# The last image of a two-layer attention kernel: output by plain stores of sums formed on chip instead of accumulating DMAs, and a reordered preparation

## The chip, the cores and the metric

The kernel runs on one core of one Trainium2 chip. A core has a matrix engine (PE, TensorE), a vector engine (DVE, VectorE), an activation engine (ACT, ScalarE), a general engine (POOL, GpSimd), and a queue engine (SP, SyncE) that issues most of the DMAs. Each engine works through its own instructions in order and waits on semaphores for the others. SBUF is the memory on the chip, PSUM the eight banks into which PE writes, and HBM, where inputs and outputs lie, is reached by DMA only. The metric is the time of one execution on the device in microseconds (us); lower is better.

## The reference

x has the shape (8, 512, 64, 64): eight images of 512 channels and N = 4096 positions. Two layers follow one another.

Layer 0 is softmax attention. With f = Wf x and pooled g = maxpool(Wg x), v = maxpool(Wh x) (1024 pooled positions):

```
s = f^T g;  beta = softmax(s);  o = v beta^T;  x1 = gamma * (Wv o) + x
```

Layer 1 is linear attention on x1, with the feature map delu(u) = 10 relu(u) + exp(10 min(u, 0)):

```
Qf = delu(wq x1);  Kf = delu(wk x1);  V = wv x1
KV   = sum over positions of Kf V^T
norm = 1 / (Qf^T (sum over positions of Kf + 1e-10))
out  = x1 + gamma * (Qf^T KV) * norm
```

Everything is float32. KV and the sum of Kf run over a whole image, so the addend of layer 1 (called C below) can be formed only when x1 of the whole image is known.

## The kernel before

The positions of an image are cut into 8 chunks of 512 (CH), 64 chunks in all (TOTAL), numbered s. A tile of a chunk has 128 partitions (channels within a group) and 4 groups (KT) of 512 positions: 1 MB. The function `step(s)` writes out one step of a software pipeline by hand: each piece of work is registered with a time inside the step, `at(t, fn, ...)`, and at the end of the step all pieces are issued in order of those times. The times only set the order in which instructions stand in each engine's queue. The loop runs over s from -9 to 71, and three images overlap in it:

- *A work* for chunk s + 9: the projections f, g and h of layer 0.
- *B work* for chunk s: the softmax attention of layer 0 (`attend`), the projection that turns the chunk's tile of x (`x_b[s]`, pool `xb`, one buffer) into x1 in place (`project`), its store to `out` by SP (line 534), and the features q and k of layer 1 (`features`, `features_exp`, `features_sum`). The q features of two chunks (a pair) lie in one tile, `qq[pair]`, half of the partitions each.
- For layer 1, x1 and the k features are turned so that positions lie on the partitions, and `gather` (line 621) adds k^T x1 of the chunk to G, which grows over an image. For all chunks but the last, x1 is turned by DMA transposes (`split_x`, `turn_halves`, `join_x`); for chunk 63, by PE (`turn_x`, line 601) with ACT copying the four results out of PSUM (line 604).
- *C work* for the image before: `start_kb` forms the matrix kb of the sums of the k features; `turn_G` turns G on PE (line 663), copies it on ACT (665) and adds its two halves into gT on DVE (671); `make_KV` multiplies it with wv, which `load_wv1` loads (638), into pkv (685), and DVE makes kv of it (691, 692); `normalize` forms the divisors of a pair on PE (703), positions along the free axis and repeated on 64 partitions, inverts all 128 x 512 of them on DVE (707) and scales qq (708); `finish` multiplies kv and qq into pa (732), ACT copies pa into a tile y of two channel groups of two chunks (735), and POOL issues a DMA of 1 MB that adds y to `out` in HBM (738).

For images 0 to 6 the C work lies under the steps of the following image. For image 7 nothing follows: after step 63 come steps 64 to 71 with C work alone, all four pairs normalized in step 64 at the times

```
at(3.6 if here else 0.2, turn_k, s - 1)
gather(s - 1, at, 0.3, 0.4)
turn_G(b_c, at, 21.2 if here else 6.0)
make_KV(b_c, at, 36.9 if here else 8.2)
for i, t in enumerate((5.79, 5.8, 12.0, 12.1)):
    normalize(pair + i, at, t, t + 1.3)
```

and finished in the odd steps 65 to 71, with two y buffers of pool `yc` and two more (`y_late`) in the buffer that held the softmax weights E. At the end a flag is read that decides whether the whole is run again in a general form; it is not in this data.

Of the kernel before, what the change touches and what calls it, by code (L numbers as in the profile page):

```python
# [35 lines left out]
F32 = mybir.dt.float32  # L36
U16 = mybir.dt.uint16
AF = mybir.ActivationFunctionType
ALU = mybir.AluOpType
# [10 lines left out]
def tile_two_attention_blocks(  # L50
# [113 lines left out]
    def run(ctx, general):  # L164
# [13 lines left out]
        def bank(name):  # L178
            return psum.tile([P, CH], F32, tag="m", name=name)

        def scratch(name):
            return temp.tile([P, CH], F32, tag="t", name=name)
# [25 lines left out]
        fgs, fs, vps = {}, {}, {}  # L208

        th, hs, es, sums, totals, rtots, te, os_, to, ns = ({} for _ in range(10))  # L210
        kTs, xTs, pks, qq, halves, turned_halves = ({} for _ in range(6))


# [381 lines left out]
            u = turned_halves[s, k].rearrange("p (h t) c -> p h t c", h=2)  # L595
            nc.scalar.copy(v[:, k], u)  # L596

        def turn_x(s, t):
            px = bank(f"px_{s}_{t}")
            for k in range(KT):  # L600
                nc.tensor.transpose(px[:, bass.ts(k, P)], x_b[s][:, k, bass.ts(t, P)], ident)
            if t == 0:
                xTs[s] = turned.tile([P, NT, C], F32, tag="xT", name=f"xT_{s}")
            nc.scalar.copy(xTs[s][:, t, :], px)

        def turn_k(s):
            pt = bank(f"pkT_{s}").rearrange("p (t n) -> p t n", n=P)
# [5 lines left out]
        def gather(s, at, t, t_out):  # L613

            b, j = divmod(s, NCHUNK)
            G, m = st[b]["G"], {}

            def product():
                pg = m["pg"] = bank(f"pg_{s}")
                for t in range(NT):  # L620
                    nc.tensor.matmul(  # L621
                        pg[half(t % 2), :], kTs[s][:, t, :], xTs[s][:, t, :],
                        start=(t < 2), stop=(t >= NT - 2),
                    )

            def out():
                if j == 0:
                    nc.vector.tensor_copy(G, m["pg"])
                else:
                    nc.vector.tensor_tensor(G, G, m["pg"], ALU.add)  # L630

            at(t, product)
            at(t_out, out)


        def load_wv1(b):
            w = st[b]["w_v1"] = yc.tile([P, KT, C], F32, tag="y", name=f"w_v1_{b}")
            nc.sync.dma_start(out=w, in_=wv1r)

        def start_kb(b):  # L640
# [56 lines left out]
        def normalize(pair, at, t, t_out):  # L697

            m = {}

            def product():
                m["pd"] = bank(f"pd_{pair}")
                nc.tensor.matmul(m["pd"], kb, qq[pair], start=True, stop=True)

            def out():
                rn = scratch(f"rn_{pair}")
                nc.vector.reciprocal(rn, m["pd"])
                nc.vector.tensor_tensor(qq[pair], qq[pair], rn, ALU.mult)

            at(t, product)  # L710
            at(t_out, out)

        def finish(pair, ks, at, t):

            b, jp = divmod(pair, NCHUNK // 2)
            m = {}

            def product():
                kv = st[b]["kv"]
                if b == B - 1 and ks[0] > 0:  # L720

                    if "late" not in st:
                        st["late"] = work1.tile([P, 2, 2, 2, CH], F32, tag="E", name="y_late")
                    y = st["late"][:, pair % 2]
                else:
                    y = yc.tile([P, 2, 2, CH], F32, tag="y", name=f"y_{pair}_{ks[0]}")
                m["y"] = y
                for i, k in enumerate(ks):
                    for e in range(2):
                        pa = bank(f"pa_{pair}_{k}_{e}")  # L730
                        hf = half(1 - e)
                        nc.tensor.matmul(  # L732
                            pa, kv[hf, bass.ts(k, P)], qq[pair][hf, :], start=True, stop=True
                        )
                        nc.scalar.copy(y[:, i, e, :], pa)  # L735

            def out():
                nc.gpsimd.dma_start(  # L738
                    out=outr[b, :, ks[0] : ks[0] + 2, bass.ts(jp, 2 * CH)],
                    in_=m["y"].rearrange("p k e n -> p k (e n)"), accum_op=ALU.add,  # L740
                )

            at(t, product)
            at(t + 3.4, out)


        def step(s):
            here, after = 0 <= s < TOTAL, 0 <= s + 1 < TOTAL
            a = s + LEAD
            b, j = divmod(s, NCHUNK)  # L750
            b_c = b - 1
            c_here = 0 <= b_c < B
            pair = (b_c * NCHUNK + j) // 2
            work = []

            def at(t, fn, *args):
                work.append((t, len(work), fn, args))

            if here:
                at(0.5, load_b, s)  # L760
            if 0 <= a and a + 2 < LEAD:
                at(0.0, load_a, a + 2)
            if LEAD <= a + 1 < TOTAL:
                at(38.5, load_a, a + 1)
            if c_here and j == 0:
                at(0.6, load_wv1, b_c)

            if here:
                attend(s, at, {
                    1: (0.0, None), 2: (1.7, 3.5), 3: (3.9, None), 6: (14.4, 16.1), 5: (16.2, 20.5),  # L770
                    7: (17.9, 21.8), 4: (19.6, 22.5),
                })
                at(-0.6, sums_of_e, s, 3)
                at(0.3, sums_of_e, s, 4)
            if 0 <= s - 1 < TOTAL:
                at(-0.5, features_exp, s - 1)
                at(-0.4, features_sum, s - 1)
                if s < TOTAL:
                    at(-0.45, join_x, s - 1, 1)
                    at(1.8, join_x, s - 1, 2)  # L780
                    at(2.3, join_x, s - 1, 3)
                at(3.6 if here else 0.2, turn_k, s - 1)
                if here:
                    gather(s - 1, at, 12.6, 13.5)
                else:
                    gather(s - 1, at, 0.3, 0.4)
            if c_here and j == 0:
                at(0.2, start_kb, b_c)
                turn_G(b_c, at, 21.2 if here else 6.0)
                make_KV(b_c, at, 36.9 if here else 8.2)  # L790
            if c_here and here and j == 0:
                normalize(pair, at, 5.6, 13.2)
            if c_here and here and j % 2 == 1 and j < NCHUNK - 1:
                normalize(pair + 1, at, 3.5, 4.9)
            if c_here and not here and j == 0:
                for i, t in enumerate((5.79, 5.8, 12.0, 12.1)):
                    normalize(pair + i, at, t, t + 1.3)
            if c_here and j % 2 == 1:
                finish(pair, (0, 1), at, 9.2)
                finish(pair, (2, 3), at, 10.9)  # L800
            if 0 <= a < TOTAL:
                a_h(a, at, 19.7, 30.8, 37.8)
                a_fg(a, at, 21.3)
            if 0 <= a - 1 < TOTAL:
                at(18.5, bias_v, a - 1)
                at(36.8, a_turn, a - 1)
                if a % NCHUNK == 0:
                    at(39.0, sums_of_v, (a - 1) // NCHUNK)
            if after:
                n = s + 1  # L810
                at(5.7, weigh_two, n, 0)
                at(7.5, weigh_two, n, 2)
                for m, t in ((2, 9.3), (4, 10.6), (6, 11.8), (8, 13.1)):
                    at(t, sum_of_e, n, m)
                at(16.1, total, n)
                at(17.0, invert, n)
                if not general:
                    at(21.5, look, n)
                at(24.3, normalize_block, n, 0, 1)
                at(26.0, normalize_block, n, 0, 0)  # L820
                at(27.3, normalize_block, n, 1, 1)
                at(29.2, normalize_block, n, 1, 0)
                at(33.6, sums_of_e, n, 1)
                at(36.0, sums_of_e, n, 2)
            if here:
                project(s, at, 24.8, 36.0)
                at(37.0, features, s)
                if s < TOTAL - 1:
                    for k in range(KT):
                        at(32.9 + k, split_x, s, k)  # L830
                        at(33.0 + k, turn_halves, s, k)
                    at(37.3, join_x, s, 0)
                else:
                    for t in range(NT):
                        at(40.4 + t * 0.45, turn_x, s, t)

            for _, _, fn, args in sorted(work, key=lambda w: w[:2]):
                fn(*args)

        load_a(0)  # L840
        load_a(1)
        for s in range(-LEAD, TOTAL + NCHUNK):
            step(s)

    ENGINES = {
# [53 lines left out]
```

## Time and profile before

| what | value |
|---|---|
| median of 3 runs | 2845.95 us (2843.32 to 2849.13) |
| the profiled execution: its own time | 2846.64 us |
| its span in the trace | 2844.9 us |
| busy: PE, DVE, ACT, POOL | 2695.6, 2144.2, 1516.6, 709.6 us |
| last PE work of the features of chunk 63 (pk) | 2764.31 to 2768.01 us |
| kv of the last image ready | 2794.05 us |
| first and last of the eight last accumulating DMAs issued | 2797.95, 2824.54 us |
| plain store of xb, issue to landing | 5.0 us |
| accumulating DMA of y, issue to landing | 11.2 us (the last four of y_late: 17.7 us) |

All times inside the trace are from the start of the span. In a line of the timeline stand the start, the time from the first start to the last end, engine and line, operation, out<-in, and the count, then in brackets how long the engine was idle before it and what ended that. One float32 matmul stands as two instructions. In a row of a table of stretches stand the busy times of the engines, then the granted clock of PE (1.00 is full), the busy share of the 16 DMA engines and the GB/s moved. In the chain of waits, "issue" is time for which the profile shows no wait.

### The profile page before, as it was taken

To read this page: it belongs to the slowest core of one execution; us is meant where nothing else is said; L and a number is where in the kernel's file an instruction comes from. 1 tells how busy PE (TensorE), PEld (TensorE's weight loads), DVE (VectorE), ACT (ScalarE), POOL (GpSimd) and SP (SyncE) were. 2 spreads that over 40 slices of the span, in tenths; PEclk is the share of its full clock that TensorE was granted. 3 is DMA by queue.
4 is the path that set the end of the run, shared out by engine and by line. 5 is a ranking of instruction groups with operands and counts; after the bars stand their busy time and mean duration, and the time that the engine had idled before them with its cause. 6 is when DMAs were issued, how large, how long until landed. Compare 5 with 4: busy or idle time off the path is not lost.

```text
span 2844.9 us, 30593 instructions
## 1 busy us (share of the span) xinstructions
PE 2695.6 (95%) x10928; PEld 1810.9 (64%) x10928; DVE 2144.2 (75%) x2982; ACT 1516.6 (53%) x2629; POOL 709.6 (25%) x552
## 2 busy tenths in 40 slices
PE   8899999999999999999999999999999999989984
PEld 6566666666666666666766666666666666655551
DVE  4678778777787777877777877877878777787752
ACT  2255555556556556556556556456555556655542
POOL 4312222222321223222231222322222222211111
PEclk9999999999999999999999999999999999999996
DMA  4143244455454446454455454445544445544456
GB/s 155 36 119 91 88 119 133 97 140 148 115 137 119 108 129 163 98 139 120 118 133 148 106 131 131 120 120 148 118 120 135 118 118 148 133 101 110 112 138 119
DMA packets 394434, 346.96 MB, mean 122 GB/s; under 512 B 274592, under 2 KB 275104, under 8 KB 394272
## 3 DMA queue, kind: packets, MB, share of 16 engines
q1 hardware_dynamic: 371712, 275.82, 34.4%
q0 software_dynamic: 17408, 67.11, 12.7%
q10 hardware_dynamic: 5152, 1.97, 0.3%
q8 instruction: 89, 1.46, 0.2%
q14 instruction: 73, 0.60, 0.1%
HBM read 144.58 MB, written 134.22 MB: 98 GB/s over the span
## 4 chain that ended last, share of the span: by engine, by line
PE 71%; DVE 10%; ACT 8%; issue 4%; DMA 2%; POOL 2%; DVEq 0%; POOLq 0%; ACTq 0%
PE M L444 22%; PE N L507 11%; PE H L283 11%; PE fg L239 7%; PE pk L554 6%; PE s L354 5%; ACT n L517 3%; PE pa L732 3%; DVE r L394 3%; ACT E L358 3%; DMA u<-w 2%; PE tot L401 2%; PE pg L621 2%; DVE r L392 2%; ACT w L583 1%
## 5 line engine op out<-in xcount | busy, mean ns | idle before, releaser
L520 POOL TENSOR_TENSOR xb<-xb,n 128x512 f32<-128x512 f32 x192 | 244.5, 1274 | 596.4 <-ACT n L517 542.9
L444 PEld LDWEIGHTS M<-T,S 128*128 128x128 f32 x1536 | 287.3, 190 | 115.9 <-issue 30.7
L596 ACT COPY xT<-u 128x1024 uint16<-128x1024 uint16 x252 | 336.1, 1343 | 44.3 <-DMA u<-w 42.7
L444 PE MATMUL M<-T,S 128*128 128x256 f32 x1536 | 359.7, 384 | 0.0
L583 ACT COPY w<-xb 128x1024 uint16<-128x1024 uint16 x252 | 244.8, 1042 | 157.3 <-DVE xb L528 157.3
L517 ACT ACTIVATE n<-N,gb_v 128x256 f32<-128x256 f32 x384 | 161.5, 473 | 308.5 <-PE N L507 308.4
L420 DVE TENSOR_TENSOR E<-E,rtot 128x1024 f32<-128x1024 f32 x256 | 304.7, 1213 | 2.4 <-ACT tot L411 1.6
L358 ACT ACTIVATE E<-s 128x512 f32<-128x512 f32 x512 | 257.6, 626 | 42.6 <-PE s L354 42.1
L523 DVE TENSOR_TENSOR xb<-xb,N 128x512 f32<-128x512 f32 x256 | 175.1, 684 | 129.8 <-POOL xb L520 127.5
L507 PE MATMUL N<-to,w_v 128*128 128x256 f32 x1024 | 251.3, 389 | 15.0 <-ACT n L517 10.7
L392 DVE TENSOR_TENSOR r<-E 128x1024 f32<-128x1024 f32 x64 | 78.4, 1225 | 226.6 <-ACT E L358 226.6
L554 PE MATMUL pk<-xb,w_kqk 128*128 128x512 f32 x512 | 235.9, 604 | 10.5 <-DVE xb L528 10.5
L738 POOL DMA_DIRECT2D out_dram<-y x60 | 72.3, 1206 | 678.0 <-ACT y L735 675.8
L354 PE MATMUL s<-f,g 64*128 64x512 f32 x1024 | 239.7, 603 | 0.7 <-ACT kT L611 0.6
L406 DVE RECIPROCAL rtot<-tot 128x512 f32<-128x512 f32 x64 | 215.4, 3365 | 27.6 <-PE tot L401 27.6
L410 ACT ACTIVATE tot<-tot 128x512 f32<-128x512 f32 x64 | 37.2, 582 | 371.6 <-DVE rtot L406 364.5
L507 PEld LDWEIGHTS N<-to,w_v 128*128 128x128 f32 x1024 | 190.0, 191 | 66.5 <-ACT n L517 40.3
L444 PE MATMUL M<-E,vT 128*128 128x256 f32 x1024 | 231.6, 379 | 0.5 <-ACT vT L331 0.5
L272 POOL TENSOR_TENSOR tha<-xa 128x512 f32<-128x512 f32 x58 | 77.0, 1327 | 619.6 <-PE M L444 605.8
L444 PEld LDWEIGHTS M<-E,vT 128*128 128x128 f32 x1024 | 194.5, 190 | 54.0 <-issue 19.8
L507 PE MATMUL N<-o,w_v 128*128 128x256 f32 x768 | 195.1, 390 | 30.2 <-ACT n L517 27.3
L239 PE MATMUL fg<-xa,w_fg 128*128 128x512 f32 x464 | 210.6, 597 | 0.0
(129 smaller groups left out, 4647.0 us busy)
## 6 DMA issues: line engine op xcount, KB each, us to landing
xb<-in_x_dram SPq DMA_DIRECT2D x64, 1024.0 KB, 7.1
out_dram<-xb SPq DMA_DIRECT2D x64, 1024.0 KB, 5.0
out_dram<-y POOLq DMA_DIRECT2D x60, 1024.0 KB, 11.2
xa<-in_x_dram SPq DMA_DIRECT2D x58, 1024.0 KB, 6.6
w_v<-in_L_conv_wv_dram SPq DMA_DIRECT2D x8, 1024.0 KB, 9.1
x_early<-in_x_dram SPq DMA_DIRECT2D x6, 1024.0 KB, 5.4
out_dram<-y_late POOLq DMA_DIRECT2D x4, 1024.0 KB, 17.7
u<-w SPq DMA_TRANSPOSE x252, 3.3
```

Source lines behind the costliest of these rows:

```text
L239: nc.tensor.matmul(fg, w_fg[:, k, :], x_a[a][:, k, :], start=(k == 0), stop=(k == KT - 1))
L283: nc.tensor.matmul(m[i], w_h7[i][:, k, :], th[a][i][:, k, :], start=(k == 0), stop=(k == hk - 1))
L354: nc.tensor.matmul(sc[e], g[half(e), i, :], fs[s][half(e), :], start=True, stop=True)
L358: nc.scalar.activation(es[s][:, 2 * i + e, :], sc[e], AF.Exp)
L420: nc.vector.tensor_tensor(b, b, r, ALU.mult)
L444: nc.tensor.matmul(m[i], v7[i][:, k, :], te[s][i][:, k, :], start=(k == 0), stop=(k == hm - 1))
L507: nc.tensor.matmul(a[:, k, :], w_v7[i][:, bass.ts(k, P)], b, start=not more and k == 0, stop=True, skip_group_check=more or k > 0,)
L517: nc.scalar.activation(u[:, k, :], m[1][:, k, :], AF.Identity, bias=gb_v0[:, c : c + 1])
L520: nc.gpsimd.tensor_tensor(of_x(*ij), of_x(*ij), u, ALU.add)
L554: nc.tensor.matmul(pk, w_kqk[:, i, e * D : (e + 2) * D], x_b[s][:, i, :], start=(i == 0), stop=(i == KT - 1),)
L583: nc.scalar.copy(w, x_b[s][:, k, :].bitcast(U16).rearrange("p (n h) -> p h n", h=2))
L596: nc.scalar.copy(v[:, k], u)
```

## The change

The C work of image 7 (chunks 56 to 63) gets functions of its own.

- x1 of chunks 56 to 62 is loaded back from `out` into tiles that are free by then: 56 into the `xa` buffer, 57 and 58 into eight small tiles w and u, 59 and 60 into T1 to T4, 61 and 62 into E. The loads stand on SP from the end of step 62 to the end of step 63. x1 of chunk 63 is still in its `xb` tile.
- The addend pa is added to x1 on the chip: three channel groups on DVE straight from PSUM, the fourth by an ACT copy and an add on POOL. Then SP stores the chunk with plain DMAs. The eight accumulating DMAs of this image and the y tiles in E go.
- The divisors are formed with positions on the partitions: 16 small matmuls of 2 columns, two reciprocals of 128 x 16, then a broadcast copy on ACT and four transposes on PE per pair, and one multiplication on DVE.
- The copies of the turned x1 of chunk 63 come after exp and relu, two of four on DVE. gT stands on DVE behind the small reciprocals and before the scaling of qq.
- wv for image 7 is loaded in step 60, into the tile of an earlier image's vT.

```diff
-        def turn_x(s, t):
-            px = bank(f"px_{s}_{t}")
-            for k in range(KT):
-                nc.tensor.transpose(px[:, bass.ts(k, P)], x_b[s][:, k, bass.ts(t, P)], ident)
-            if t == 0:
-                xTs[s] = turned.tile([P, NT, C], F32, tag="xT", name=f"xT_{s}")
-            nc.scalar.copy(xTs[s][:, t, :], px)
+        def turn_x(s):
+            pxs[:] = [bank(f"px_{s}_{t}") for t in range(NT)]
+            for t in range(NT):
+                for k in range(KT):
+                    nc.tensor.transpose(pxs[t][:, bass.ts(k, P)], x_b[s][:, k, bass.ts(t, P)], ident)
+
+        def copy_x(s):
+            xTs[s] = turned.tile([P, NT, C], F32, tag="xT", name=f"xT_{s}")
+            for t in range(NT):
+                if t < NT // 2:
+                    nc.vector.tensor_copy(xTs[s][:, t, :], pxs[t])
+                else:
+                    nc.scalar.copy(xTs[s][:, t, :], pxs[t])
...
+        def place(s, *tiles):
+
+            b, j = divmod(s, NCHUNK)
+            x_last[s] = []
+            for t in tiles:
+                k, n = len(x_last[s]), t.shape[1]
+                nc.sync.dma_start(out=t, in_=outr[b, :, k : k + n, bass.ts(j, CH)])
+                stored.setdefault(s, []).append((t, k, n))
+                x_last[s] += [t[:, i, :] for i in range(n)]
...
+        def divisors(pair):
+
+            if "d" not in late:
+                late["d"] = bank("d").rearrange("p (i t e) -> p i t e", t=NT, e=2)[:, 0 : NCHUNK // 2]
+            for t in range(NT):
+                nc.tensor.matmul(
+                    late["d"][:, pair % (NCHUNK // 2), t, :], qq[pair][:, bass.ts(t, P)],
+                    kb[:, 0:P:D], start=True, stop=True,
+                )
+
+        def invert_divisors(n):
+            if n == 0:
+                late["rd"] = small.tile([P, NCHUNK // 2, NT, 2], F32, tag="rd", name="rd")
+            i = slice(2 * n, 2 * n + 2)
+            nc.vector.reciprocal(late["rd"][:, i], late["d"][:, i])
+
+        def spread(pair):
+
+            u = scratch(f"u_{pair}")
+            r = late["rd"][:, pair % (NCHUNK // 2)].rearrange("p t e -> p (t e)")
+            nc.scalar.copy(
+                u.rearrange("p (i d) -> p i d", d=D), r.unsqueeze(2).to_broadcast([P, 2 * NT, D])
+            )
+            sp = late[pair] = bank(f"sp_{pair}")
+            for t in range(NT):
+                nc.tensor.transpose(sp[:, bass.ts(t, P)], u[:, bass.ts(t, P)], ident)
+
+        def scale(pair):
+            nc.vector.tensor_tensor(qq[pair], qq[pair], late[pair], ALU.mult)
+
+        def finish_last(pair, k):
+            b, jp = divmod(pair, NCHUNK // 2)
+            for e in range(2):
+                pa = bank(f"pa_{pair}_{k}_{e}")
+                hf = half(1 - e)
+                nc.tensor.matmul(
+                    pa, st[b]["kv"][hf, bass.ts(k, P)], qq[pair][hf, :], start=True, stop=True
+                )
+                x = x_last[2 * pair + e][k]
+                if k < KT - 1:
+                    nc.vector.tensor_tensor(x, x, pa, ALU.add)
+                else:
+                    y = scratch(f"y_{pair}_{e}")
+                    nc.scalar.copy(y, pa)
+                    nc.gpsimd.tensor_tensor(x, x, y, ALU.add)
+
+        def store_last(s):
+            b, j = divmod(s, NCHUNK)
+            for t, k, n in stored[s]:
+                nc.sync.dma_start(out=outr[b, :, k : k + n, bass.ts(j, CH)], in_=t)
...
+            first = TOTAL - NCHUNK
+            if s == TOTAL - 4:
+                at(30.0, load_wv1, B - 1)
+            if s == TOTAL - 2:
+                at(37.3, place_first, first)
+            if s == TOTAL - 1:
+                at(0.7, place_small, first + 1, "w")
+                at(5.0, place_small, first + 2, "u")
+                at(22.0, place_half, first + 3, "T2", "T3")
+                at(22.1, place_two, first + 5)
+                at(36.9, place_half, first + 4, "T1", "T4")
+            if s == TOTAL:
+                pairs = [first // 2 + i for i in range(NCHUNK // 2)]
+                x_last[s - 1] = [x_b[s - 1][:, k, :] for k in range(KT)]
+                stored[s - 1] = [(x_b[s - 1], 0, KT)]
+                at(-0.45, copy_x, s - 1)
+                at(0.1, turn_k, s - 1)
+                at(0.2, start_kb, B - 1)
+                gather(s - 1, at, 0.25, 0.35)
+                at(0.4, divisors, pairs[0])
+                at(0.5, divisors, pairs[1])
+                turn_G(B - 1, at, 0.6)
+                at(0.7, invert_divisors, 0)
+                at(0.8, divisors, pairs[2])
+                at(0.9, divisors, pairs[3])
+                at(1.1, invert_divisors, 1)
+                at(1.2, spread, pairs[0])
+                at(2.2, scale, pairs[0])
+                make_KV(B - 1, at, 3.0)
+                at(3.1, spread, pairs[1])
+                at(3.2, scale, pairs[1])
+                for i in range(2, 4):
+                    at(6.6, spread, pairs[i])
+                for i, p in enumerate(pairs):
+                    for k in range(KT):
+                        at(7.0 + 4 * i + k, finish_last, p, k)
+                    if i < 2:
+                        at(7.1 + 4 * i, scale, pairs[i + 2])
+                    at(10.5 + 4 * i, store_last, 2 * p)
+                    at(10.6 + 4 * i, store_last, 2 * p + 1)
...
-        for s in range(-LEAD, TOTAL + NCHUNK):
+        for s in range(-LEAD, TOTAL + 1):
```

`turn_G` registers its DVE part (gT) 1.5 after the time given to it, so at 2.1, and `make_KV` its DVE part (kv) 3.5 after, so at 6.5. The small functions that call `place` (`place_first`, `place_small`, `place_half`, `place_two`) only choose the tiles named above.

More of the change, by code (lines that the diff above doesn't have):

```diff
@@ L210, in run @@
         th, hs, es, sums, totals, rtots, te, os_, to, ns = ({} for _ in range(10))
+        pxs, x_last, stored, late = [], {}, {}, {}
         kTs, xTs, pks, qq, halves, turned_halves = ({} for _ in range(6))
@@ L636, in load_wv1 @@
         def load_wv1(b):
-            w = st[b]["w_v1"] = yc.tile([P, KT, C], F32, tag="y", name=f"w_v1_{b}")
+            if b < B - 1:
+                w = yc.tile([P, KT, C], F32, tag="y", name=f"w_v1_{b}")
+            else:
+                w = image.tile([P, KT, C], F32, tag="vT", name=f"w_v1_{b}")
+            st[b]["w_v1"] = w
             nc.sync.dma_start(out=w, in_=wv1r)
@@ L719, in product @@
                 kv = st[b]["kv"]
[L720 to L727, printed above, removed]
+                y = m["y"] = yc.tile([P, 2, 2, CH], F32, tag="y", name=f"y_{pair}_{ks[0]}")
                 for i, k in enumerate(ks):
@@ L744, in finish, with place_first @@
             at(t + 3.4, out)
+        def place(s, *tiles):
[6 more added lines that the diff above has]
+                x_last[s] += [t[:, i, :] for i in range(n)]
+        def place_first(s):
+            place(s, xa.tile([P, KT, CH], F32, tag="xa", name=f"x1_{s}"))
@@ new lines, in place_small, with place_half, place_two @@
+        def place_small(s, tag):
+            place(s, *(
+                work1.tile([P, 1, CH], F32, tag=f"{tag}{k}", name=f"x1_{s}_{k}") for k in range(KT)
+            ))
+        def place_half(s, *tags):
+            place(s, *(work1.tile([P, 2, CH], F32, tag=t, name=f"x1_{s}_{t}") for t in tags))
+        def place_two(s):
+            e = work1.tile([P, MT, CH], F32, tag="E", name=f"x1_{s}")
+            place(s, e[:, 0:KT, :])
+            place(s + 1, e[:, KT:MT, :])
+        def divisors(pair):
[6 more added lines that the diff above has]
+                )
@@ new lines, in scale @@
+        def scale(pair):
[11 more added lines that the diff above has]
+                    nc.vector.tensor_tensor(x, x, pa, ALU.add)
+                else:
+                    y = scratch(f"y_{pair}_{e}")
+                    nc.scalar.copy(y, pa)
+                    nc.gpsimd.tensor_tensor(x, x, y, ALU.add)
@@ L764, in step @@
                 at(38.5, load_a, a + 1)
-            if c_here and j == 0:
+            if c_here and here and j == 0:
                 at(0.6, load_wv1, b_c)
@@ L781, in step @@
                     at(2.3, join_x, s - 1, 3)
-                at(3.6 if here else 0.2, turn_k, s - 1)
+                if here:
+                    at(3.6, turn_k, s - 1)
                 if here:
                     gather(s - 1, at, 12.6, 13.5)
-                else:
-                    gather(s - 1, at, 0.3, 0.4)
-            if c_here and j == 0:
+            if c_here and here and j == 0:
                 at(0.2, start_kb, b_c)
-                turn_G(b_c, at, 21.2 if here else 6.0)
-                make_KV(b_c, at, 36.9 if here else 8.2)
+                turn_G(b_c, at, 21.2)
+                make_KV(b_c, at, 36.9)
             if c_here and here and j == 0:
@@ L794, in step @@
                 normalize(pair + 1, at, 3.5, 4.9)
[L795 to L798, printed above, removed]
+            if c_here and here and j % 2 == 1:
                 finish(pair, (0, 1), at, 9.2)
@@ L833, in step @@
                 else:
-                    for t in range(NT):
-                        at(40.4 + t * 0.45, turn_x, s, t)
+                    at(40.4, turn_x, s)
+            first = TOTAL - NCHUNK
[38 more added lines that the diff above has]
+                    at(10.6 + 4 * i, store_last, 2 * p + 1)
             for _, _, fn, args in sorted(work, key=lambda w: w[:2]):
```

## The prediction

> **What bounds the kernel now.** I read the page first (PE busy 95% of the span), then the chain of waits. Over the span the chain is 71% PE; after the last main step it is something else:
>
> ```profile
> 2761.88 1.27 POOL xb L520
> 2763.14 34.78 issue
> 2797.93 0.02 POOLq L738
> 2797.95 1.20 POOL out_dram L738
> ...
> 2824.52 1.23 POOLq L858
> ```
>
> Columns: start, length, what. From 2763 on the chain does not follow PE's stream: it is a 35 us preparation, then POOL's eight accumulating stores. The change touches this stretch and a few DMAs before it, so the prediction is made for 2763 to 2844.9. What the engines do in it, in order of time:
>
> ```profile
> 2773.73 3.63 PE L621 MATMUL pg<-xT,kT 128*64 128x512 f32 x8 [0.46 <-ACT kT L611]
> 2778.45 3.36 DVE L707 RECIPROCAL rn<-pd 128x512 f32<-128x512 f32 x1 [0.36 <-PE pd L703]
> 2782.45 3.35 DVE L707 RECIPROCAL rn<-pd 128x512 f32<-128x512 f32 x1
> 2786.45 0.75 DVE L671 TENSOR_TENSOR gT<-g 128x256 f32<-128x256 f32 x2
> 2787.30 5.44 PE L685 MATMUL pkv<-w_v,gT 128*128 128x512 f32 x8 [7.59 <-issue]
> 2792.78 0.75 DVE L691 SCALAR_TENSOR_TENSOR kv<-b_v,ksum,pkv 128x512 f32<-128x512 f32 x1 [5.58 <-PE pkv L685]
> 2822.19 2.05 ACT L735 COPY y_late<-pa 128x512 f32<-128x512 f32 x4 [3.69 <-DMA out_dram<-y_late]
> ```
>
> G^T (L671) was ready to be formed at 2780.34, when ACT's copy of it ended, but stands on DVE behind two reciprocals of 3.36 us. PE is idle 7.6 us meanwhile. kv is ready at 2794.05. The last line shows ACT waiting for a y buffer that an accumulating DMA still reads: from 2797.95 the DMA sets the pace. Stretches of the same trace:
>
> ```profile
> core 0: us, PE busy (x) PEld busy (x) DVE busy (x) ACT busy (x) POOL busy (x), PEclk, DMA share, GB/s
> 2766.00:2767.50 1.50, 1.50 (x5) 0.65 (x4) 0.00 (x0) 0.00 (x0) 0.00 (x0) 1.00 1.03 362
> 2770.40:2773.80 3.40, 0.70 (x6) 0.49 (x8) 1.85 (x9) 2.35 (x5) 0.00 (x0) 1.00 0.45 167
> 2773.80:2777.20 3.40, 3.40 (x8) 0.67 (x8) 0.03 (x1) 0.00 (x0) 0.00 (x0) 0.50 0.00 0
> 2784.00:2787.50 3.50, 0.20 (x1) 0.23 (x2) 3.17 (x4) 0.00 (x0) 0.00 (x0) 0.51 0.00 0
> 2787.50:2790.90 3.40, 3.40 (x5) 1.33 (x6) 0.00 (x0) 0.00 (x0) 0.00 (x0) 0.50 0.00 0
> 2800.00:2841.00 41.00, 12.09 (x40) 5.34 (x36) 2.00 (x2) 11.80 (x24) 8.35 (x7) 0.64 1.04 205
> ```
>
> The engines of the DMA are full (share 1.04) at 205 GB/s while they accumulate; with the plain store of xb alone (2766.0 to 2767.5) they are as full at 362 GB/s. The 8.39 MB of accumulation take 41.7 us of DMA records (2799.72 to 2841.45, 5.2 us per MB), and from the last byte to the end of the span it is 3.4 us. The two half-clock rows show why pg and pkv are slow: pg is 8 in 1.94 us one step earlier, and pkv is 3.6 us on average for the seven images before.
>
> **What the Trainium skill says.** "DMA: Bandwidth & Descriptors", SWDGE vs HWDGE vs iDMA: accumulating is possible only in a DMA issued from GpSimd, a plain store may go from SP; "Issuing engines are not separate DMA queues": all share 16 engines. The trace agrees (the accumulation is on q0, everything of SP on q1), so what the change gains is the rate, not a second path. "TensorE: Matmul & The Clock Gate", Part 1: after an idle window of about 3.4 us the clock is halved, after a busy one it is full, and the windows run free. The trace agrees: 0.70 us busy in 3.4 was followed by clock 0.50. "SBUF — State Buffer", Who interferes with whom: a VectorE instruction with one SBUF input does not contend with GpSimd. The new adds read x1 from SBUF and pa from PSUM; the trace has no such pair side by side long enough to tell.
>
> **The change, part by part** (times on the clock of the trace before; pk of chunk 63 ends at 2768.0 in both).
>
> 1. Exp and relu go before the copies of x^T, and two of four copies go to DVE. Exp and relu take 1.30 us (2770.46 to 2771.76) and now end at 2769.35. DVE copies from 2768.54: 2 x 0.69 (the G copy, L628), overlapped by 0.05, so 2769.85. kk 0.69: 2770.55, before 2772.48. ACT's other two copies (2 x 0.51) end at 2770.4, under kk.
> 2. k^T 0.63 on PE, 0.4 on ACT, then pg. PE's gap is now about 2 us with 0.6 of work in it, before 4 with as little; I take the full clock: 1.94 us, end 2773.7 (half: 3.63). G added at 2774.5, before 2778.1.
> 3. Divisors of pairs 0 and 1 stand before G^T on PE: 8 matmuls of two passes each. No row has them; a transpose pass with a weight load is 0.12 us (16 in 1.91), a weight load of pd alone 0.19. 16 x 0.12 to 0.19 = 1.9 to 3.0, I take 2.4: 2776.1. pGT 0.6, ACT 0.6: 2777.35.
> 4. Before gT, DVE now has the second small reciprocal, which waits for pairs 2 and 3 on PE behind pGT: 2.4 more, 2779.1. A reciprocal of 16 elements a row is 16/512 of 3.36 plus the 0.15 of the smallest DVE rows: 0.25. gT 0.75: 2780.2, before 2787.2. So the wait on 6.7 us of reciprocals becomes one of about 2 us on small matmuls.
> 5. pkv: PE has been busy, so full clock, 3.6: 2783.9. Scaling of pair 1 stands before kv on DVE and waits for its transposes behind pkv: 0.6 + 0.7. kv 1.27: **2786.5, before 2794.05, 7.5 us earlier**. All 13.4 us of L707 go. The broadcast copies on ACT (0.5 to 1.3 each) lie under the divisors and pkv; the first would be seen only above 1.7.
> 6. Finish: 24 adds and 2 scalings on DVE at 0.65 (L523: two in 1.33), 17.2 us, ready at 2804.3; k=3 goes by ACT (0.51) and POOL (L520, 1.27), 10.2 us for eight, beside DVE. PE: 32 of 0.45. Chunk 56 needs six DVE operations and pa number 7: 2786.5 + 3.2 + 0.6 + 1.3 = 2791.6.
> 7. Stores: first data 0.9 after issue (xb: 2764.68 to 2765.59), 2792.6. 1.05 MB at 362 GB/s is 2.9; store and load together took 7.0 for two, 3.5. I take 3.1: 8 x 3.1 = 24.8, 2817.4. Chunks of pair p are ready every 4.6 us and drain in 6.2, so the DMA does not starve. With the 3.4 us of ending: **2820.8**.
> 8. Moved DMAs. x1 of chunk 56 now stands on SP before the load of xb 63: at most 3.8 us of delay (one load's records, 2742.91 to 2746.7). xb 63 then lands near 2750.5; POOL first needs it at 2757.06: hidden, 6.5 us to spare. The loads of 57 to 62 share the DMA with the two accumulations issued at 2746.8 and 2749.1: 7 loads, xb in and out at 3.1, and 12.1 of accumulation, from 2742.5: done by 2783, before 2787. Loads that wait for T2, T3 hold up on SP only other loads and the store of xb 63, which nobody reads until pair 3. w_v of the last image goes behind xb of step 60, 30 us before the next transposes: nothing, as it was hidden in the tail too (landed 2773, used 2787).
>
> Sum: kv 7.5; first data 7.1 earlier (2799.7 to 2792.6); drain 41.7 to 24.8, 16.9; together 24.0 off the span of 2844.9. The profiled run took 2846.64; the median is 2845.95, so I take the difference from the median: 2821.9.
>
> **Rivals.**
> *A, DMA drain with early kv* (above): 2822, own range 2816 to 2827 (2.8 to 3.5 us per MB). For it: full DMA in both kinds of row.
> *B, half clock in the preparation*: windows run free, so pg (+1.7) and pkv (+1.8 to 3.6) may be slow again, and the divisors may cost 0.19 a pass (+1.2): kv 2791 to 2793, time 2826 to 2828. Against: PE's gaps are shorter than in the row at 0.70.
> *C, x1 loads collide in step 63*: if xb 63 comes over 6.5 us late or the transposes of chunk 62 slow down, the step stretches by the rest; at half the DMA rate 3 to 6 us: 2825 to 2828. Against: SP's ring was empty from 2746.7 to 2765.6.
> *D, slower: stores serialized on SP.* If each waited for the one before to land: 5.0 per 1 MB store, by estimate 2.7 per quarter (2.0 of fixed time, 5.0 less 3.0, plus a quarter of 2.9) and 3.5 per half: 5 + 8 x 2.7 + 4 x 3.5 + 15 = 56 us from 2791.7, then the ending: about 2850 on the span, 2851. It decides against the change from 6.1 us per MB (2844.9 - 3.4 - 2792.6 = 48.9 for 8 MB). Against: in the built order a store waits for the eighth DMA before it, not the last.
> *E, no difference*: the gain would have to be spent elsewhere; nothing in the trace offers 24 us.
>
> **Chances.** A 0.74, B 0.12, C 0.09, D 0.03, E 0.02. Faster 0.95, same 0.02, slower 0.03; 0.2% (5.7 us, the spread of the three runs) is about what can be told. The range 2814 to 2829 takes in A with 2.7 us per MB and an earlier kv below, B and C above.
>
> **What will show it.** Right: gT right after the small reciprocals near 2780; L707 gone from the tail; kv near 2786.5; SP stores back to back with DMA share 1 at 330 to 370 GB/s; last byte about 3 us before the end. Wrong: PE clock 0.5 over pg or pkv; holes between the stores; DVE adds waiting for x1; step 63's first xb add after 2758.

## The result and the profile after

| | before | after |
|---|---|---|
| median of 4 runs, us | 2847.52 (2843.32 to 2849.13) | 2825.07 (2822.93 to 2826.77) |
| the profiled execution: its own time, us | 2846.64 | 2822.93 |
| its span, us | 2844.9 | 2821.1 |

The ratio is 0.9923 (95% interval 0.9906 to 0.994): 22 us faster. On the spans it is 23.8 us, against the 24.0 that were forecast. A second set of five runs of the changed kernel gave a median of 2822.18 beside a before of 2847.78, ratio 0.9914 (0.99 to 0.9927).

Until the last main step is over nothing has moved: pk of chunk 63 ends at 2768.83, before at 2768.01. In the kernels below that moment lies between 2765 and 2771, without order, so stretches of the tail are given **from the end of pk** ("pk +") wherever two kernels are compared.

The timeline of PE after the change, from the turned x1 of chunk 63 on (start, time from first start to last end, engine and line, operation, out<-in, count, in brackets the idle time before and what ended it):

```profile
2769.76 0.82 PE L603 MATMUL px<-ident,xb 128*128 128x128 f32 x6
2771.41 0.63 PE L616 MATMUL pkT<-ident,kk 128*128 128x128 f32 x4 [0.84 <-DVE kp L657]
2772.50 1.94 PE L628 MATMUL pg<-xT,kT 128*64 128x512 f32 x8 [0.46 <-ACT kT L618]
2774.37 1.95 PE L782 MATMUL d<-kb,qq 128*128 128x2 f32 x16
2776.18 0.64 PE L674 MATMUL pGT<-ident,G 128*128 128x128 f32 x4
2776.67 2.25 PE L782 MATMUL d<-kb,qq 128*128 128x2 f32 x16
2778.78 1.09 PE L802 MATMUL sp<-ident,u 128*128 128x128 f32 x4
2779.92 6.18 PE L696 MATMUL pkv<-w_v,gT 128*128 128x512 f32 x8
```

PE has no hole of over 0.9 us left up to pkv, pg is at its full-clock 1.94 us, and the reciprocals of 3.36 us are gone from before gT. But pkv, which starts 8.2 us earlier, takes 6.18 us, longer than the 5.44 of before. The table of stretches (busy time of PE, PEld, DVE, ACT, POOL, then PE's granted clock, DMA share, GB/s) says why:

```profile
2770.40:2773.80 3.40, 2.10 (x12) 0.90 (x12) 2.04 (x10) 1.89 (x4) 0.00 (x0) 1.00 1.05 392
2774.50:2778.00 3.50, 3.50 (x32) 3.41 (x32) 0.94 (x2) 1.15 (x3) 0.00 (x0) 1.00 1.01 391
2778.20:2785.00 6.80, 6.75 (x14) 3.46 (x14) 1.55 (x4) 1.40 (x3) 0.00 (x0) 0.50 0.01 5
2795.23:2818.77 23.54, 8.57 (x37) 4.98 (x33) 10.13 (x17) 3.42 (x6) 7.78 (x7) 0.79 0.98 361
```

PE's records fill 3.50 of 3.50 us in the second row, all of them divisors and pG^T, and yet PE's granted clock is at half in the third. That is looked into below. The last row is the whole drain: the DMA engines are full at 361 GB/s, where the accumulation was full at 205. The DMA table for 2785 to 2822, in 40 slices (tenths of busy share, then GB/s):

```profile
DMA  0000000000099999999999999999999999930000
GB/s 0 0 0 0 0 18 0 0 0 0 0 359 383 381 383 383 388 376 381 379 363 376 374 350 390 350 388 372 374 379 387 370 383 394 363 148 11 0 0 0
```

There is no hole between the first byte and the last: the eight chunks' stores run back to back. Chunk 56 is issued by SP at 2794.31 and its data starts at 2795.23; the last byte lands at 2818.77, 2.3 us before the end. The chain of waits no longer helps here. For this kernel it goes back only over the last adds and has 0.0% of the span:

```profile
2804.68 0.69 DVE xb L817
2805.37 0.34 POOLq L976
2805.71 0.69 POOL xb L821
```

It starts from POOL's last work (the add for chunk 63) and doesn't see that 12 us of plain stores are still under way. The end of this kernel is read from the DMA table.

From pk +, in us, all kernels of this document, each from one profiled execution ("end" is the start of the last instruction of the trace, 0.05 us before the span ends):

| kernel | pkv takes | kv ready | data of the drain: first, last | drain takes | end |
|---|---|---|---|---|---|
| before | 5.44 | 26.03 | 31.70, 73.43 | 41.73 | 76.79 |
| after | 6.18 | 19.61 | 26.40, 49.94 | 23.54 | 52.25 |
| after, again | 5.60 | 19.59 | 26.38, 49.95 | 23.57 | 52.25 |
| e1_prep_only | 5.01 | 19.57 | 24.98, 66.46 | 41.48 | 69.68 |
| e2_stores_only | 5.28 | 25.59 | 32.60, 58.53 | 25.93 | 61.06 |
| e3_gt_first | 3.63 | 21.35 | 27.18, 68.99 | 41.80 | 72.33 |
| e4_half_stored | 5.72 | 19.59 | 24.28, 39.30 | 15.03 | 46.87 |
| e5a_late_divisors | 4.78 | 15.87 | 25.42, 48.77 | 23.35 | 51.05 |
| e5b_filled | 3.60 | 14.88 | 24.43, 47.76 | 23.33 | 49.96 |
| e6_first_in_pieces | 5.63 | 19.59 | 22.43, 46.75 | 24.31 | 48.96 |
| e7_all | 3.60 | 14.88 | 17.73, 44.69 | 26.95 | 46.79 |
| e8_steady | 3.60 | 14.88 | 17.91, 45.17 | 27.27 | 47.77 |

The 24.5 us between the first two rows' ends are 5.3 of an earlier first byte, 18.2 of a shorter drain and 1.0 of a shorter ending.

### The profile page after: what moved, and what is told of

It is laid out like the page before. It is cut to its first block, busy times and chain, and to the rows that moved or that the text cites. A ratio compares the mean times of both kernels' runs of the same rounds, so it can differ in the third digit from the quotient of the medians.

```text
span 2821.1 us, 30743 instructions
## 1 busy us (share of the span) xinstructions
PE 2695.8 (96%) x10968; PEld 1817.2 (64%) x10968; DVE 2148.3 (76%) x3006; ACT 1506.6 (53%) x2607; POOL 709.9 (25%) x552
```

## The experiments

Theory A is the forecast's: the drain sets the end, its length is set by the kind of DMA, and the preparation only sets when it begins. The rival, P, looks for the larger part of the gain in the preparation. The first two runs do one half of the change each.

**The preparation alone.** From the changed kernel: no loads of x1, and the accumulating DMAs as before.

```diff
-                        at(7.0 + 4 * i + k, finish_last, p, k)
...
-                    at(10.5 + 4 * i, store_last, 2 * p)
-                    at(10.6 + 4 * i, store_last, 2 * p + 1)
+                    finish(p, (0, 1), at, 7.0 + 4 * i)
+                    finish(p, (2, 3), at, 8.0 + 4 * i)
```

> The changed preparation (copies after exp and relu, divisors with positions on partitions, G^T ahead of the scaling), but the eight accumulating DMAs of the kernel before. Theory A (the DMA drain sets the end, the preparation only says when it starts): kv about 5.6 us earlier than before, as in the changed kernel; the first y tile 3.9 us later; then 41.7 us of accumulation and 3.4 us of ending as before: span 2839 to 2840, 5 to 6 us below the 2844.9 of before, ratio about 0.998. Rival P (the preparation, with the 13.4 us of reciprocals taken off VectorE, is what gained): span 2821 to 2828.

Median 2840.86, ratio 0.9972 (0.9965 to 0.9979), 7.1 us, a little more than the 5 to 6 expected. kv comes 6.5 us earlier, the first data 6.7, and the end 7.1. The accumulation takes 41.48 us, as before (41.73), though it starts 6.7 us earlier.

**The stores alone.** The changed kernel with the old preparation: copies of the turned x1 on ACT before exp and relu, 128 x 512 divisors and reciprocals.

```diff
+                normalize(pairs[0], at, 5.79, 7.09)
+                normalize(pairs[1], at, 5.8, 7.1)
+                turn_G(B - 1, at, 6.0)
+                make_KV(B - 1, at, 8.2)
+                normalize(pairs[2], at, 12.0, 15.9)
+                normalize(pairs[3], at, 12.1, 19.9)
```

> x1 loaded back, adds on chip and plain stores as in the changed kernel, but the preparation of the kernel before (reciprocals of 128 x 512; those of pairs 2 and 3 stand on VectorE after the adds of pairs 0 and 1, so that the first stores don't wait for them). Theory A: kv at 2794 to 2795; first store data near 2800; VectorE has 8.1 us of reciprocal and scaling between the adds, so pairs 1 and 2 come every 8 us where the drain takes 6: last data near 2827, span 2829 to 2831, 14 to 16 us below before. Rival P: span not more than 7 us below before (2838 or more).

Median 2831.55, ratio 0.9943 (0.9927 to 0.996), 16.4 us by the medians and 15.7 in the tail. So the two halves give 7.1 and 15.7, together 22.8 of the 24.5: the stores carry two thirds of it, and A holds. The 1.7 left over lies in the drain: it takes 25.93 us here and 23.54 in the changed kernel, 2.4 more, of which the times of the first bytes take some 0.5 back. DVE in this run, from its timeline:

```profile
2797.59 3.68 DVE L814 TENSOR_TENSOR x<-x,pa 128x512 f32<-128x512 f32 x6 [1.50 <-PE pa L809]
2801.19 3.35 DVE L715 RECIPROCAL rn<-pd 128x512 f32<-128x512 f32 x1
...
2808.17 0.68 DVE L814 TENSOR_TENSOR x_T<-x_T,pa 128x512 f32<-128x512 f32 x1
2808.77 3.35 DVE L715 RECIPROCAL rn<-pd 128x512 f32<-128x512 f32 x1
```

The two reciprocals of pairs 2 and 3 stand between the adds, so sums come late and the DMA runs short:

```profile
2803.10:2829.00 25.90, 12.66 (x37) 6.38 (x36) 16.85 (x22) 3.47 (x6) 7.96 (x7) 0.76 0.89 327
```

A share of 0.89 at 327 GB/s over the drain, where the changed kernel has 0.98 at 361. With the accumulation the same kind of reciprocals cost the drain next to nothing: 41.73 us with them (before) and 41.48 without (e1_prep_only).

What "the stores" stands for is more than one thing. The accumulating DMAs add to HBM, are issued by POOL and move their 8.39 MB in 2176 packets; the plain ones are issued by SP and have 4352. No run changes one of these alone (a plain store issued by POOL, for one), so it is shown that the kind of DMA sets the rate, and not which of its traits does.

**One number.** How much of the preparation's 7.1 us was only the order of the work? The kernel before, with G^T ahead of the reciprocals:

```diff
-                turn_G(b_c, at, 21.2 if here else 6.0)
+                turn_G(b_c, at, 21.2 if here else 5.5)
```

> The kernel before with one number changed: turn_G of the last image at 5.5 instead of 6.0, so that the transposes of G stand before the divisors on TensorE and G^T before the reciprocals on VectorE. Theory A: G^T at about 2780; pkv then runs under the two reciprocals, which end near 2788; kv near 2789.4, 4.7 us earlier; the accumulations start that much earlier: span 2840, ratio about 0.998. A rival (the reciprocals of pairs 0 and 1 must come before the first pa anyway, so the order does not matter): kv and span as before within 1 us.

Median 2843.51, ratio 0.9985 (0.9976 to 0.9993): 4.5 us. Its timeline (PE and DVE):

```profile
2781.87 1.88 PE L703 MATMUL pd<-qq,kb 128*128 128x512 f32 x4
2782.69 0.76 DVE L671 TENSOR_TENSOR gT<-g 128x256 f32<-128x256 f32 x2 [1.37 <-ACT g L665]
2783.37 3.35 DVE L707 RECIPROCAL rn<-pd 128x512 f32<-128x512 f32 x1
2783.59 3.63 PE L685 MATMUL pkv<-w_v,gT 128*128 128x512 f32 x8
2791.35 0.74 DVE L691 SCALAR_TENSOR_TENSOR kv<-b_v,ksum,pkv 128x512 f32<-128x512 f32 x1
```

The reciprocals now run beside pkv instead of ahead of it. And pkv takes 3.63 us, the full clock: ahead of it stand the old divisors with 512 columns, not the new ones with two. What the full clock saves is lost again at L691, which waits on DVE for the second reciprocal until pk +20.1, 4.1 us after the last matmul of pkv.

**The half clock.** Is it the two-column matmuls? Two runs on the changed kernel. The first thins them out ahead of pkv (pair 1's go beside pG^T, those of pairs 2 and 3 behind pkv):

```diff
-                at(0.5, divisors, pairs[1])
+                at(0.65, divisors, pairs[1])
...
-                at(0.8, divisors, pairs[2])
-                at(0.9, divisors, pairs[3])
-                at(1.1, invert_divisors, 1)
+                at(3.15, divisors, pairs[2])
+                at(7.05, divisors, pairs[3])
+                at(7.06, invert_divisors, 1)
```

with the scalings of pairs 1 to 3 moved back to fit.

> The changed kernel reordered: on TensorE the divisors of pair 1 stand behind the transposes of G, those of pairs 2 and 3 behind pkv; on VectorE the second small reciprocal and the scaling of pair 1 stand behind kv. Theory A with small matmuls that don't keep the clock up (H): G^T 9.1 us after pk (changed kernel 11.0), pkv from 9.7, still at half clock for most, 5 to 6.2 us, kv at 16 to 17.2 (changed kernel 19.6), end 2.4 to 3.6 us earlier, 48.6 to 49.8 after pk. Rival (any matmul keeps the clock up; the half clock of pkv came from PE's waits before it): pkv at full clock, 3.6 us, kv at 14.6, end near 47.3.

The second adds two matmuls of 512 columns whose result nobody reads, where PE waits for the reciprocal:

```diff
+                at(0.9, filler, 2)
```

(`filler(n)` issues `matmul(f, ident, kk)` n times into a free bank f.)

> As e5a_late_divisors, with two matmuls of 128x512 (0.9 us) into an unused bank in the gap of TensorE before the transposes of pair 0; nothing waits for them. Theory H (only columns that stream count for the clock): they raise the activity of the window before pkv, pkv takes 3.6 to 4.5 us, kv 14.6 to 15.5 us after pk, end near 47.3 to 48. Rival (the clock follows the busy time of the records, full there already): pkv as in e5a_late_divisors, end the same within 0.5 us, or later by the time of the two matmuls.

The timelines of PE, first without and then with the filler:

```profile
2778.59 1.12 PE L802 MATMUL sp<-ident,u 128*128 128x128 f32 x4 [1.00 <-ACT u L797]
2779.50 4.78 PE L696 MATMUL pkv<-w_v,gT 128*128 128x512 f32 x8
```

```profile
2777.89 1.96 PE L780 MATMUL filler<-kk,ident 128*128 128x512 f32 x4
2779.69 0.60 PE L807 MATMUL sp<-ident,u 128*128 128x128 f32 x4
2780.13 3.60 PE L696 MATMUL pkv<-w_v,gT 128*128 128x512 f32 x8
```

With the fillers PE's granted clock stays 1.00 over the whole preparation and pkv takes 3.60 us, here and in the two combined kernels below that have them too. Without them, with 16 small passes ahead of pkv, the clock still falls, at pk +8.7, but comes back after 3.4 us, in the middle of pkv (0.65 over its first 3.4 us). So thinning the passes out shortened the half clock and did not prevent it.

The 6.18 us of the changed kernel's trace should not be read alone. Four more kernels of the table have the same 32 passes ahead of pkv (the second run of the changed kernel, e1, e4 and e6), and there it takes 5.01 to 5.72. In all five the clock is at half for 6.8 us. In the four it falls earlier, at pk +8.1 to +8.8 where it was +9.3, so that it slows the second half of the divisors as well, and pkv starts later. The extreme is e1_prep_only:

```profile
2775.23 3.37 PE L788 MATMUL d<-kb,qq 128*128 128x2 f32 x16
2779.61 5.01 PE L696 MATMUL pkv<-w_v,gT 128*128 128x512 f32 x8
```

In all five pkv ends at pk +17.2 to +17.3 and kv is ready at +19.6: what the half clock takes from the one it leaves to the other.

The fillers also close the hole of 1.00 us that the first of the two runs has before sp, so filling the hole and streaming wide columns are not separated by this pair alone. But the changed kernel has no such hole, and its clock falls all the same; what it lacks is wide matmuls. Two kinds of narrow work are not separated either: among the passes ahead of the fall stand the four transposes of G with 128 columns, 0.64 us of it.

The times don't follow. Medians 2821.5 and 2821.68, ratios 0.991 (0.9894 to 0.9927) and 0.9908 (0.9892 to 0.9925), which the noise does not separate from the changed kernel's. kv is 3.7 and 4.7 us earlier, but the ends, 51.05 and 49.96, only 1.2 and 2.3, and both later than expected: the divisors put off to behind pkv now stand on PE among the products of pair 0, and chunk 56's data starts 9.55 us after kv instead of 6.8. The gain was given back between kv and the first store.

**An earlier first store.** The changed kernel, chunks 56 and 57 stored a channel group at a time, each behind its add:

```diff
+                    if i == 0:
+                        for k in range(KT):
+                            at(7.5 + k, store_piece, 2 * p, k)
+                            at(7.6 + k, store_piece, 2 * p + 1, k)
+                        continue
```

> The changed kernel, but chunk 56 is stored in four pieces of 256 KB, and the pieces of chunks 56 and 57 stand on SP in the order in which their adds end. Theory A (the drain sets the end): the first store is issued after the first add (near 2790.5) and not after the POOL add of the chunk (2794.3), the drain starts up to 3.8 us earlier; while TensorE delivers one pa in 0.9 us at half clock the drain, 0.73 us a piece, may starve a little: span 2 to 4 us below the changed kernel's 2821.1. Rival (the adds on VectorE and POOL, or the end of the program, set the end): within 1 us of 2821.

Median 2820.33, ratio 0.9903 (0.9887 to 0.992). The drain starts 4.0 us earlier, takes 0.8 longer (24.31), and the end comes 3.3 earlier. A's reading, that the start of the drain passes through to the end, holds but for that 0.8.

**Half the bytes.** To see whether anything else lies closely under the drain, this run stores only channel groups 0 and 1 of image 7 (the final groups 2 and 3 are left out):

```diff
+                if k < 2:
+                    n = min(n, 2)
+                    nc.sync.dma_start(..., in_=t[:, 0:n, :])
```

> The changed kernel with only channel groups 0 and 1 of each of the eight last chunks stored at the end (4.2 of 8.4 MB); all adds stay. Left out: the final values of groups 2 and 3 of image 7, where x1 stays in the output. Theory A (the drain sets the end): the end comes when the last stored piece is ready and landed: the second group's add of chunk 63 ends 35.3 us after pk, 0.5 MB more 3 to 4 us, the ending 2.3: end 41 to 42 us after pk (changed kernel 52.25), 10 to 11 us off. Rival (the adds on VectorE and POOL, which end 37.6 us after pk, or latencies behind them, set the end): not more than 3 us off.

Median 2816.45, ratio 0.9894 (0.9874 to 0.9913). The data ends 10.6 us earlier, but the end only 5.4: between the last byte and the end there are now 7.6 us, not 2.3. Neither size expected above is met; there is a second floor. On POOL, from the timeline:

```profile
2803.16 1.27 POOL L821 TENSOR_TENSOR x<-x,y 128x512 f32<-128x512 f32 x1 [1.08 <-ACT y L820]
2804.39 1.26 POOL L821 TENSOR_TENSOR xb<-xb,y 128x512 f32<-128x512 f32 x1
```

The last add of POOL ends at 2805.65 and the last instruction of the trace starts at 2814.97, 9.3 us later. No kernel here ends sooner after POOL's last work (the nearest are 10.4 us in e8_steady and 11.1 in e2_stores_only; it is 14.7 in the changed kernel). What lies between shows in the instructions that close the program (line 1015 of this run: count, then shortest, median and longest in ns, then first and last start):

```profile
L1015 POOLq DRAIN  x3: 44/107/2687, 2811.2 to 2814.8; - x3
L1015 SPq DRAIN  x3: 7/7/13, 2811.8 to 2814.5; - x3
```

SP is through at 2811.9; POOL's first DRAIN takes 2.69 us, to 2813.9, and the common end follows. In the changed kernel the same DRAIN of POOL is over at 2813.8 and SP's comes only at 2820.2, behind the last store. So in this run POOL's own ending sets the end, and in the changed kernel SP's does. Why POOL needs 8.2 us from its last add to the end of that DRAIN stays open.

**All together.** The late divisors, the fillers and the pieces in one kernel, and then a version that spreads the small work otherwise (the divisors of pairs 2 and 3 right behind pkv, scalings between the sums):

> e5b_filled together with the first two chunks stored in pieces as in e6_first_in_pieces. Theory A: the gains add up, as both only move the start of the drain: kv at 14.6 to 15.5 us after pk, the drain from 2.9 us later, 24.3 us of it, 2.2 of ending: end 44 to 45 us after pk, 7 to 8 us below the changed kernel's 52.25; a time of 2816 to 2819. Rival (a new wait takes the gain: pieces that starve behind the late divisors and transposes on TensorE): the drain starts early but takes 27 us or more, end as in e5b_filled.

Median 2818.92 (2814.49 to 2825.41), ratio 0.991 (0.9893 to 0.9927). The drain starts 8.7 us earlier than in the changed kernel, takes 3.4 longer, and the end comes 5.5 earlier, at 46.79 where 44 to 45 was expected. The DMA share over the drain is 0.86: DVE and PE can no longer deliver sums as fast as the stores take them.

The edit of the second version, against that kernel:

```diff
-                at(3.15, divisors, pairs[2])
-                at(7.05, divisors, pairs[3])
-                at(7.06, invert_divisors, 1)
+                at(3.15, divisors, pairs[3])
+                at(6.6, invert_divisors, 1)
+                at(9.05, spread, pairs[1])
...
-                at(3.1, spread, pairs[1])
-                at(6.6, scale, pairs[1])
+                at(3.1, divisors, pairs[2])
+                at(10.15, scale, pairs[1])
...
-                    at(8.05, spread, pairs[i])
+                    at(11.05, spread, pairs[i])
...
-                        at(9.1 + 2 * i, scale, pairs[i + 2])
+                        at(13.1 + i, scale, pairs[i + 2])
```

> As e7_all, but the divisors of pairs 2 and 3 stand on TensorE right behind pkv, under the making of kv, and the transposes and scalings of pairs 1 to 3 behind the adds of the pairs before, so that the first pieces come without gaps. Theory A: the first data 0.5 us later than in e7_all (18.2 us after pk against 17.7), but the drain takes 24.3 to 25 us instead of 26.95: end 44.6 to 45.5 us after pk, 1.3 to 2.2 below e7_all's 46.8 and 7 us below the changed kernel's 52.25. Rival (a floor under the drain, seen in e4_half_stored where the end came 9.3 us after POOL's last add whatever was stored): POOL's last add at about 35 us after pk, end not below 44.3; then the gain stops near there.

It missed. The drain takes 27.27 us, and PE waits twice for a scaling on DVE:

```profile
2785.63 1.13 PE L817 MATMUL pa<-qq,kv 64*128 64x512 f32 x4 [0.99 <-DVE qq L810]
...
2792.01 7.14 PE L817 MATMUL pa<-qq,kv 64*128 64x512 f32 x32 [1.45 <-DVE qq L810]
```

Median 2819.2 (2814.67 to 2822.35), ratio 0.9906 (0.9891 to 0.9921). The changed kernel ran once more beside it:

> The changed kernel as it is, beside the improved version on the same chip. Both theories: end 52 us after pk, ratio to before 0.991 to 0.9925.

Its median was 2822.18, ratio 0.9914 (0.99 to 0.9927), and its tail ends at pk +52.25, to the hundredth where it ended before. The tails of the two combined kernels are 4.5 to 5.5 us shorter; the whole times are 3 us lower by the medians, and the intervals of the ratios overlap. That they beat the changed kernel is shown for the tail, in one profiled execution of each, not for the whole time.

Not tried: plain stores issued by POOL, stores made to wait for one another (rival D), other counts of filler matmuls, and an earlier end of POOL's adds.

## Why the prediction was right, step by step

The forecast, 2821.9, stands 3.2 us under the median of the first runs and 0.3 under that of the second, and A is the case that came true, with half of B in it. Its times counted from pk's end, beside those of the changed kernel:

| step | forecast | measured |
|---|---|---|
| 1: kk ready | 2.55 | 2.43 |
| 2: pg ends | 5.7 (full clock) | 5.61 (full clock) |
| 3: 16 passes of divisors | 2.4 us | 1.95 and 2.25 us |
| 4: gT ready | 12.2 | 10.99 |
| 5: pkv takes | 3.6 us | 6.18 us |
| 5: kv ready | 18.5 | 19.61 |
| 7: first data | 24.6 | 26.40 |
| 7: drain takes | 24.8 us | 23.54 us |
| 7: last byte to the end | 3.4 us | 2.32 us |
| the end | 52.8 | 52.25 |

*Steps 1 to 4* held. Of the bounds 0.12 to 0.19 us a pass, the lower was the truer: 0.12 a pass for the first 16, all at full clock, where 0.15 was taken; the second 16, the end of them at half clock, took 0.14. That gT came 1.2 us early is mostly this, in this trace: in the other four with the same preparation the half clock made the second 16 passes 2.69 to 3.37 us long, and gT came at 11.43 to 12.11. The 128 x 16 reciprocal took 0.26 us, estimated at 0.25.

*Step 5* failed in its clock: "PE has been busy, so full clock". PE was busy by its records, and the clock was at half; pkv cost 2.6 us more (1.4 to 2.1 in the other four traces, where the divisors lost the rest), and kv came 1.1 us late in all five. The prediction had named it as a sign of being wrong: "PE clock 0.5 over pg or pkv". This is the second half of rival B, which was given 0.12: its pg was at full clock, its pkv was not. Its bound of 1.8 to 3.6 held the 2.6. "TensorE: Matmul & The Clock Gate", Part 1, of the Trainium skill says that the clock is set "based on how busy the PE has been recently"; the trace agrees only if busy is not what the records show, since 3.50 of 3.50 us of records, all of them passes of two or 128 columns, were followed by a clock of 0.50.

*Step 6* was short by 0.7 us: the first add starts 1.28 us after kv where 0.6 was counted. The adds themselves ran at a pitch of 0.60 us beside POOL's, which took 1.27 as before; neither was slowed by the other.

*Step 7* was too dear by 1.3 us. 23.54 us for 8.39 MB are 2.94 us per 1.05 MB, against the 3.1 taken, between the 2.9 of a store alone and the 3.5 of a store beside a load. The 3.4 us of ending was read from an accumulating DMA; after the plain stores it is 2.3. Both terms are sizes, not mechanisms. Late by 1.8 at the first byte and early by 2.3 after it, the sum came out 0.5 us from the truth. That these misses cancelled is luck; the terms were less exact than the total, and it is the mechanism, a shorter drain of plain stores behind an earlier kv, that the runs confirm.

*Step 8* held: POOL's first add into xb 63 starts at 2757.86, 10.97 us before pk's end, and before the change at 2757.06, 10.95 before it. The loads that were moved into step 63 cost nothing, and rival C fell. Rival D fell with the DMA table: no hole between stores. As "DMA: Bandwidth & Descriptors" of the Trainium skill has it, under "Issuing engines are not separate DMA queues", the gain is no second path: the 16 engines are full before and after, and what changed is how long the same bytes keep them, 41.5 to 41.8 us for 8.39 MB in the three accumulating kernels and 23.3 to 23.6 in the plain ones that don't starve.

## What to carry to other kernels

Where a full DMA sets the end, look at its GB/s, not its share: an accumulating DMA was as full at 205 GB/s as a plain store at 361, and adding on engines that are idle anyway bought the difference. Once the drain is fast, work that the slow one covered comes into sight (here reciprocals among the adds, then small matmuls among the products), so an earlier start must be paid for in steadiness, and only part of it reaches the end. An engine that ends its work under the last transfer may have an ending of its own close behind it.

## What the runs showed of the hardware that was not expected

- Matmuls with two columns filled PE's records and didn't hold its clock: 32 passes and four transposes in 4.5 us, then half clock for 6.8 us, in five traces, with pkv at 5.01 to 6.18. Two matmuls of 512 columns ahead of pkv, whose result is thrown away, brought it to 3.60; behind 512-column divisors it took 3.63.
- Accumulating into HBM from POOL took 1.77 times as long as plain stores of the same bytes from SP (41.73 to 23.54 us for 8.39 MB), with the DMA engines full in both.
- From the last byte to the end of the span it is 3.2 to 3.4 us after accumulating DMAs issued on POOL and 2.1 to 2.6 after plain stores on SP; with little left to store the end came 9.3 us after POOL's last add, set by a DRAIN of POOL that took 2.69 us.
